# Layer-0 scores by query strips: 32 queries of four heads to a product, in place of 128 queries of one head

## The chip, the cores and the metric

The kernel runs on one core of a Trainium2 chip. A core has a matrix engine (TensorE, PE in the profile; its weight loads stand apart as PEld), a vector engine (VectorE, DVE), a scalar engine (ScalarE, ACT), a general engine (GpSimd, POOL) and a queue engine (SyncE, SP) that issues most transfers here. Engines work through their own instruction queues in order and wait for each other by semaphores. TensorE reads its operands from SBUF and writes to PSUM banks; of a matmul's two operands one is loaded first (the stationary one, `lhsT`), the other (the moving one, `rhs`) streams past it. The metric is the time of one execution on the device, in microseconds.

## What is computed

Two transformer layers over 1024 tokens of 512 features, each with an attention part and a feed-forward part, with layer norms, shifts, scales and gates around them. Only the first layer's attention bears on the change. It has 32 query heads and 8 key/value heads of 128 features, four query heads to one key/value head:

```python
q = _dequant_matmul(hidden_states, qw_q, scales_q).reshape(b, s, NH, HD).transpose(0, 2, 1, 3)
k = _dequant_matmul(hidden_states, qw_k, scales_k).reshape(b, s, NKV, HD).transpose(0, 2, 1, 3)
v = _dequant_matmul(hidden_states, qw_v, scales_v).reshape(b, s, NKV, HD).transpose(0, 2, 1, 3)
q = _apply_rope(q, cos, sin)
k = _apply_rope(k, cos, sin)
k = jnp.repeat(k, rep, axis=1)
v = jnp.repeat(v, rep, axis=1)
scores = jnp.einsum('bhqd,bhkd->bhqk', q, k) / math.sqrt(HD)
causal = jnp.tril(jnp.ones((s, s), dtype=bool))
scores = jnp.where(causal[None, None], scores, jnp.finfo(scores.dtype).min)
attn = jax.nn.softmax(scores.astype(jnp.float32), axis=-1).astype(q.dtype)
ctx = jnp.einsum('bhqk,bhkd->bhqd', attn, v)
ctx = ctx.transpose(0, 2, 1, 3).reshape(b, s, NH * HD)
return _dequant_matmul(ctx, qw_o, scales_o)
```

All of it is in float32; the weights come as small integers with scales and are made into floats on the core. The mask is causal: query i sees keys 0 to i.

## The kernel before

Layer 0's attention is a loop over 8 groups `g` (one key/value head and its four query heads) and, in each, over the 8 query blocks `qi` of 128 queries, in the order 7, 0, 6, 1, 5, 2, 4, 3 (in the last group 3, 7, 2, 6, 1, 5, 0, 4). One pair (g, qi) is a step; there are 64. A step works on the keys up to the block's end, n = qi + 1 blocks of 128, so it has 128(qi + 1) key columns.

A step first calls `head_probs(u, r)` for the four heads r (L314 to L336). For a head, TensorE multiplies the 128 queries of the block with all key columns, in pieces of up to 512 (L320), into a PSUM tile `sc` of two banks, of which there are three. VectorE adds the causal mask `cmask` to the last 128 columns (L325), and takes the negated maximum of each row (L327). ScalarE takes the exponential with the row's sum (L330), VectorE the reciprocal (L335), and ScalarE scales by it (L336). The probabilities stand in one wide tile `pr` for all four heads. `transpose_probs` (L338) then transposes it in squares of 32 x 32, a quarter at a time (L342), and 16 transfers on SP's queue (L344) put the pieces together in `pT`, keys on partitions. `pr` and `pT` have one buffer each for the large blocks (qi from 4 on) and one for the small.

Two steps later `context` (L349) multiplies `pT` with the values, 128 keys at a time, for the four heads at once (L353), ScalarE copies the result to `ctxT` (L359), and `project_o` multiplies it with the output weights (L364), VectorE applies the gate (L369) and GpSimd adds to the tokens (L370). In the program these stand after heads 1 and 3 of the step in hand (`drain`).

`side_work(g, i)` prepares the next group during step i: weights are loaded and made into floats by VectorE (`dequant`, L218), and `project_k`, `project_v`, `project_q` multiply them with the layer-normed tokens `hT`. `project_rope` (L229) does a head in two halves of 512 tokens: four matmuls (L234), three VectorE products with cosine and sine (L240, L242, L243), and a GpSimd addition (L244) that writes the half of the rotated head. Step 3 projects heads 0 and 1 of the next group, step 5 head 2, step 7 head 3. Each head has its own tile `qT` of 128 x 1024, eight of them in rotation:

```python
qp = st.enter_context(tc.tile_pool(name="a0q", bufs=8))
...
qT[h] = qp.tile([P, S], F32, tag="qT", name="qT")
project_rope(qT[h], wf.pop(("q", h)))
```

The lines give each engine's work in program order; when the program is built, instructions of different engines and, within an engine, of neighbouring parts are interleaved, so that for instance a context matmul can stand ahead of scores that stand above it in the source. What follows from that on the chip is fixed: each engine runs its list in order. A float32 matmul appears in the profile as two records, with two weight loads.

Of the kernel before, what the change touches and what calls it, by code (L numbers as in the profile page):

```python
# [9 lines left out]
F32 = mybir.dt.float32  # L10
# [3 lines left out]
ALU = mybir.AluOpType  # L14
AX = mybir.AxisListType
PSUM = bass.MemoryType.PSUM

P = 128
S = 1024
# [4 lines left out]
NEG = -1e30  # L24
# [3 lines left out]
REP = NH // NKV  # L28
# [14 lines left out]
def block_kernel(ctx: ExitStack, tc: tile.TileContext, a: dict, out: bass.AP):  # L43
    nc = tc.nc

    const = ctx.enter_context(tc.tile_pool(name="const", bufs=1))
# [18 lines left out]
    def psum_mm():  # L65

        return psA[0].tile([P, 512], F32, tag="mm", name="mm")
# [23 lines left out]
    make_identity(nc, ident)  # L91
    cmask = const.tile([P, P], F32, tag="cmask", name="cmask")
    make_causal_mask(nc, cmask, mask_val=NEG)
    eps_t = const.tile([P, 1], F32, tag="eps", name="eps_t")
    nc.vector.memset(eps_t, EPS)

# [93 lines left out]
    with ExitStack() as st:  # L190
# [7 lines left out]
            hT = layernorm_mod(hp, mod[0, 0], mod[0, 1])  # L198
        wp = st.enter_context(tc.tile_pool(name="a0w", bufs=3))
        kvp = st.enter_context(tc.tile_pool(name="a0kv", bufs=2))  # L200
        qp = st.enter_context(tc.tile_pool(name="a0q", bufs=8))
        rp = st.enter_context(tc.tile_pool(name="a0r", bufs=2))
        pp = st.enter_context(tc.tile_pool(name="a0p", bufs=1))
        tmp_open(st, "a0", bufs=2)
# [4 lines left out]
        B = 32  # L209
        NB = P // B  # L210
# [18 lines left out]
        def project_rope(dst, wf):  # L229

            for half in range(2):
                ps = psum_mm()
                for c in range(NC):
                    nc.tensor.matmul(  # L234
                        ps, lhsT=wf[:, c, :], rhs=hT[half][:, c, :],
                        start=(c == 0), stop=(c == NC - 1),
                    )
                sl = bass.ts(half, 512)
                t1 = rp.tile([P, 512], F32, tag="t1", name="t1")
                nc.vector.tensor_mul(t1, ps, cosT[:, sl])  # L240
                t2 = rp.tile([P, 512], F32, tag="t2", name="t2")
                nc.vector.tensor_mul(t2[0:64, :], ps[64:128, :], sinT[64:128, sl])  # L242
                nc.vector.tensor_mul(t2[64:128, :], ps[0:64, :], sinT[0:64, sl])  # L243
                nc.gpsimd.tensor_tensor(dst[:, sl], t1, t2, ALU.add)  # L244

        kT, vv, qT, wo, wf = {}, {}, {}, {}, {}
# [6 lines left out]
        def project_k(g):  # L253
            kT[g] = kvp.tile([P, S], F32, tag="kT", name="kT")
            project_rope(kT[g], wf.pop(("k", g)))
# [23 lines left out]
            vv[g], vv[g + 1] = v[:, :, :HD], v[:, :, HD:]  # L279

        def project_q(h):
            qT[h] = qp.tile([P, S], F32, tag="qT", name="qT")
            project_rope(qT[h], wf.pop(("q", h)))

        def load_o_weight(g):
            w = wp.tile([P, REP, D], F32, tag="wo", name="wo", bufs=2)
# [9 lines left out]
        class Step:  # L296


            def __init__(self, g, qi):
                self.g, self.qi, self.n = g, qi, qi + 1  # L300
                size = "big" if qi >= NT // 2 else "small"
                cap = NT if qi >= NT // 2 else NT // 2
                shape = [P, NB * REP * cap * B]
                used = NB * REP * self.n * B
                pr = pp.tile(shape, F32, tag=f"pr{size}", name="pr")
                pT = pp.tile(shape, F32, tag=f"pT{size}", name="pT")


                self.pr, self.pT = (
                    t[:, :used].rearrange("p (b r k i) -> p b r k i", b=NB, r=REP, i=B)  # L310
                    for t in (pr, pT)
                )

        def head_probs(u, r):  # L314

            nk = u.n * P
            ps = sp.tile([P, S], F32, tag="sc", name="sc")
            for n0 in range(0, nk, 512):
                w = min(512, nk - n0)
                nc.tensor.matmul(  # L320
                    ps[:, n0 : n0 + w], lhsT=qT[u.g * REP + r][:, bass.ts(u.qi, P)],
                    rhs=kT[u.g][:, n0 : n0 + w], start=True, stop=True,
                )
            dg = ps[:, u.qi * P : nk]
            nc.vector.tensor_tensor(dg, dg, cmask, ALU.add)  # L325
            nb = small.tile([P, 1], F32, tag="nb", name="nb")
            nc.vector.tensor_reduce(nb, ps[:, :nk], AX.X, ALU.max, negate=True)  # L327
            rs = small.tile([P, 1], F32, tag="rs", name="rs")
            pr = u.pr[:, :, r, :, :]
            nc.scalar.activation(  # L330
                pr.rearrange("p b k i -> p k b i"),
                ps[:, :nk].rearrange("p (k b i) -> p k b i", b=NB, i=B),
                AF.Exp, bias=nb, accum_out=rs,
            )
            nc.vector.reciprocal(rs, rs)  # L335
            nc.scalar.activation(pr, pr, AF.Copy, scale=rs)  # L336

        def transpose_probs(u):  # L338

            for b in range(NB):  # L340
                t = u.pr[:, b, :, :, :].rearrange("p r k i -> p (r k i)")
                nc.vector.transpose(t, t)  # L342
                for q in range(NB):
                    nc.sync.dma_start(  # L344
                        u.pT[b * B : (b + 1) * B, q, :, :, :].rearrange("p r k i -> p (r k i)"),
                        t[q * B : (q + 1) * B, :],
                    )

        def context(u):  # L349

            ps = psum_mm()
            for kj in range(u.n):
                nc.tensor.matmul(  # L353
                    ps, lhsT=vv[u.g][:, kj, :],
                    rhs=u.pT[:, :, :, kj, :].rearrange("p a r i -> p r a i"),
                    start=(kj == 0), stop=(kj == u.n - 1),
                )
            u.ctxT = rp.tile([P, REP, P], F32, tag="ctxT", name="ctxT")
            nc.scalar.copy(u.ctxT.rearrange("p r q -> p (r q)"), ps)  # L359
# [12 lines left out]
        def side_work(g, i):  # L372

            if g + 1 == NKV:
                if i in (1, 3):
                    mod_chunk(1, 3 + i // 2)
                elif i == 5:
                    mod_chunk(1, 5)
                return
            h0 = (g + 1) * REP  # L380
            if i == 0:
                load_k(g + 1)
            elif i == 1:
                project_k(g + 1)
                load_q(h0)
            elif i == 2:
                if (g + 1) % 2 == 0:
                    project_v(g + 1)
                load_q(h0 + 1)
            elif i == 3:  # L390
                project_q(h0)
                project_q(h0 + 1)
                load_q(h0 + 2)
            elif i == 4:
                load_q(h0 + 3)
                if g == 3:
                    mod_prepare(1)
                for l, j in ([(0, 3 + g)] if g < 3 else [(1, g - 4)] if g > 3 else []):
                    mod_chunk(l, j)
            elif i == 5:  # L400
                project_q(h0 + 2)
            elif i == 6:
                load_o_weight(g + 1)
            else:
                project_q(h0 + 3)
# [16 lines left out]
        def drain(u, part):  # L422
            if u is not None:
                (context if part == 0 else project_o)(u)

        for g in range(NKV):
            last = g == NKV - 1
            order = (3, 7, 2, 6, 1, 5, 0, 4) if last else (7, 0, 6, 1, 5, 2, 4, 3)
            for i, qi in enumerate(order):
                u = Step(g, qi)  # L430
                old = behind.pop(0) if len(behind) == 2 else None
                for r in range(REP):
                    head_probs(u, r)
                    if r % 2:
                        drain(old, r // 2)
                transpose_probs(u)
                behind.append(u)
                side_work(g, i)
        for u in behind:
            context(u)  # L440
            project_o(u)
# [5 lines left out]
    st = ctx.enter_context(ExitStack())  # L447
# [7 lines left out]
    def bank():  # L455
        return sp.tile([P, 512], F32, tag="sc", name="sc")
# [53 lines left out]
    with ExitStack() as f0:  # L510
# [55 lines left out]
        for j in range(NF):  # L566
            for b in range(2):
                pgu = []
                for m in range(2):
                    ps = bank()  # L570
                    for c in range(NC):
                        nc.tensor.matmul(  # L572
                            ps, lhsT=gu[:, j, m, c, :], rhs=hTc[b][:, c, :],
                            start=(c == 0), stop=(c == NC - 1),
# [70 lines left out]
    B = 32  # L645
# [506 lines left out]
```

## Time and profile before

| | us |
|---|---|
| median of three runs | 1970.83 |
| the three runs | 1971.68, 1970.83, 1964.02 |
| the profiled execution | 1969.94 |
| its span, first to last instruction | 1968.2 |

| engine | busy, us | share of the span |
|---|---|---|
| TensorE, matmul | 1848.3 | 94% |
| TensorE, weight loads | 871.5 | 44% |
| VectorE | 1178.6 | 60% |
| ScalarE | 667.5 | 34% |
| GpSimd | 225.5 | 11% |

The mean granted clock of TensorE is 0.967 of full speed. Layer 0's attention ends near 1150 us; after it come layer 0's feed-forward part and layer 1.

How to read the rows shown below: a row of instructions gives the line, the engine, the operation, output<-input by the program's names (`sc` scores, `nb` negated maximum, `mm` a PSUM tile of the projections), shapes and count, then busy time and the mean duration of one in ns, then the idle time of the engine before these instructions and what ended it. A row of the timeline gives start and length in us, and in brackets the idle time before it. Busy time of TensorE has the latency of each record in it, so that records that follow each other closely overlap: how far they stand apart is read from starts.

### The profile page before, as it was taken

How to read it: one execution, taken by the hardware profiler on the slowest of the kernel's cores; microseconds unless marked ns; L12 is line 12 of the kernel's file. 1: busy time of each engine (PE TensorE's matmuls, PEld its weight loads, DVE VectorE, ACT ScalarE, POOL GpSimd, SP SyncE). 2: the span in 40 equal slices, each digit the busy share in tenths (PEclk: the TensorE clock that was granted, in tenths of full speed). 3: DMA queues.
4: the chain of work that ended last, by engine and by line, in shares of the span. 5: the costliest groups of instructions: out<-in, count | busy, mean ns of one | idle time of the engine just before them, and what ended most of it. 6: DMA issues, size and time to landing. Idle time of an engine off the chain costs nothing.

```text
span 1968.2 us, 21006 instructions
## 1 busy us (share of the span) xinstructions
PE 1848.3 (94%) x6550; PEld 871.5 (44%) x6550; DVE 1178.6 (60%) x2638; ACT 667.5 (34%) x1392; POOL 225.5 (11%) x192
## 2 busy tenths in 40 slices
PE   4989999999999999999998879999988999999987
PEld 3434454444544444544443434444554444333434
DVE  5766756677566777566776542323456667677432
ACT  1134424434334344244335410000113323354520
POOL 0211111111111111111210110002000000000010
PEclk9989999999999999999999989999999889999999
DMA  5344435345533444353444360001001000000001
GB/s 198 107 111 137 120 99 137 90 128 148 128 89 83 114 141 115 106 136 93 126 127 96 86 239 0 0 0 48 0 2 63 10 8 7 4 7 8 4 11 38
DMA packets 93424, 155.77 MB, mean 79 GB/s; under 512 B 25056, under 2 KB 37984, under 8 KB 93312
## 3 DMA queue, kind: packets, MB, share of 16 engines
q1 hardware_dynamic: 92432, 151.53, 28.6%
q0 software_dynamic: 880, 2.88, 0.4%
q8 instruction: 53, 0.87, 0.2%
q14 instruction: 59, 0.48, 0.1%
HBM read 74.38 MB, written 2.36 MB: 39 GB/s over the span
## 4 chain that ended last, share of the span: by engine, by line
PE 74%; DVE 14%; DMA 3%; ACT 3%; issue 2%; SPq 1%; POOL 1%; DVEq 0%; POOLq 0%; ACTq 0%
PE mm L234 12%; PE mm L364 10%; PE mm L353 9%; PE sc L320 8%; PE sc L572 8%; PE sc L756 5%; PE sc L805 4%; PE sc L591 4%; PE ctx L829 3%; DVE q L767 2%; PE sc L666 2%; DVE nb L327 2%; PE mm L274 2%; PE sc L974 1%; DMA os<-in_s_o_dram 1%
## 5 line engine op out<-in xcount | busy, mean ns | idle before, releaser
L330 ACT ACTIVATE pr<-sc,nb 128x1024 f32<-128x1024 f32 (+7 forms) x256 | 188.2, 737 | 416.7 <-DVE nb L327 243.4
L234 PE MATMUL mm<-hT,wf 128*128 128x512 f32 x640 | 284.1, 595 | 8.3 <-ACT wf L251 6.4
L353 PE MATMUL mm<-pT,v 128*128 128x512 f32 x576 | 267.3, 610 | 21.0 <-DMA pT<-pr 21.0
L320 PE MATMUL sc<-kT,qT 128*128 128x512 f32 (+3 forms) x768 | 275.6, 490 | 7.4 <-ACT pr L330 7.4
L364 PE MATMUL mm<-wo,ctxT 128*128 128x512 f32 x512 | 237.7, 603 | 11.4 <-ACT ctxT L359 11.2
L320 PEld LDWEIGHTS sc<-kT,qT 128*128 128x128 f32 x768 | 139.5, 191 | 159.1 <-issue 126.1
L336 ACT ACTIVATE pr<-pr,rs 128x1024 f32<-128x1024 f32 (+7 forms) x256 | 188.3, 771 | 50.0 <-DVE rs L335 49.7
L234 PEld LDWEIGHTS mm<-hT,wf 128*128 128x128 f32 x640 | 121.6, 191 | 159.6 <-issue 144.6
L327 DVE TENSOR_REDUCE nb<-sc 128x1 f32<-128x1024 f32 (+7 forms) x256 | 187.7, 751 | 3.5
L342 DVE STREAM_TRANSPOSE pr<-pr 128x1024 f32<-128x1024 f32 (+7 forms) x256 | 177.7, 747 | 19.8 <-ACT pr L336 19.2
L818 ACT ACTIVATE pspace<-sc 128x512 f32<-128x512 f32 (+3 forms) x303 | 127.0, 505 | 168.3 <-PE sc L812 120.3
L353 PEld LDWEIGHTS mm<-pT,v 128*128 128x128 f32 x576 | 111.3, 196 | 148.9 <-issue 144.0
L756 PE MATMUL sc<-kv,q 32*128 32x512 f32 (+3 forms) x768 | 157.5, 550 | 11.0 <-DVE mx L767 9.5
L767 DVE CUSTOM_DVE_ANT_0 q<-sc,cwide 128x512 f32<-128x512 f32 (+3 forms) x256 | 125.5, 490 | 67.4 <-PE sc L756 42.6
L370 POOL TENSOR_TENSOR x<-x,ot 128x512 f32<-128x512 f32 x64 | 83.2, 1299 | 669.2 <-DVE ot L369 576.6
L572 PE MATMUL sc<-hT,gu 128*128 128x512 f32 x352 | 153.1, 594 | 0.0
L364 PEld LDWEIGHTS mm<-wo,ctxT 128*128 128x128 f32 x512 | 94.6, 191 | 128.1 <-issue 92.3
L805 PE MATMUL sc<-q,kv 32*128 32x512 f32 (+3 forms) x768 | 111.5, 583 | 4.2 <-DVE mx L772 2.0
L244 POOL TENSOR_TENSOR qT<-t,t 128x512 f32<-128x512 f32 x64 | 87.6, 1368 | 182.5 <-DVE t L243 182.5
L335 DVE RECIPROCAL rs<-rs 128x1 f32<-128x1 f32 x256 | 37.7, 157 | 114.0 <-ACT pr L330 113.2
L572 PEld LDWEIGHTS sc<-hT,gu 128*128 128x128 f32 x352 | 66.2, 190 | 85.2 <-issue 79.6
L772 DVE TENSOR_REDUCE mx<-sc 128x1 f32<-128x512 f32 x128 | 79.2, 681 | 37.1 <-PE sc L756 37.1
(166 smaller groups left out, 1755.3 us busy)
## 6 DMA issues: line engine op xcount, KB each, us to landing
pT<-pr SPq DMA_DIRECT2D x128, 128.0 KB, 2.3
pT<-pr SPq DMA_DIRECT2D x128, 112.0 KB, 2.2
wm<-in_wmodT_dram SPq DMA_DIRECT2D x48, 256.0 KB, 2.8
pT<-pr SPq DMA_DIRECT2D x128, 96.0 KB, 2.1
pT<-pr SPq DMA_DIRECT2D x128, 80.0 KB, 2.1
wi<-in_qw_q_dram SPq DMA_DIRECT2D x32, 256.0 KB, 4.1
ws<-in_s_q_dram SPq DMA_DIRECT2D x32, 256.0 KB, 3.8
oi<-in_qw_o_dram SPq DMA_DIRECT2D x32, 256.0 KB, 3.5
```

Source lines behind the costliest of these rows:

```text
L234: nc.tensor.matmul(ps, lhsT=wf[:, c, :], rhs=hT[half][:, c, :], start=(c == 0), stop=(c == NC - 1),)
L320: nc.tensor.matmul(ps[:, n0 : n0 + w], lhsT=qT[u.g * REP + r][:, bass.ts(u.qi, P)], rhs=kT[u.g][:, n0 : n0 + w], start=True, stop=True,)
L327: nc.vector.tensor_reduce(nb, ps[:, :nk], AX.X, ALU.max, negate=True)
L330: nc.scalar.activation(pr.rearrange("p b k i -> p k b i"), ps[:, :nk].rearrange("p (k b i) -> p k b i", b=NB, i=B), AF.Exp, bias=nb, accum ...
L336: nc.scalar.activation(pr, pr, AF.Copy, scale=rs)
L342: nc.vector.transpose(t, t)
L353: nc.tensor.matmul(ps, lhsT=vv[u.g][:, kj, :], rhs=u.pT[:, :, :, kj, :].rearrange("p a r i -> p r a i"), start=(kj == 0), stop=(kj == u.n ...
L364: nc.tensor.matmul(ps, lhsT=u.ctxT[:, r, :], rhs=wo[u.g][:, r, :], start=(r == 0), stop=(r == REP - 1),)
L572: nc.tensor.matmul(ps, lhsT=gu[:, j, m, c, :], rhs=hTc[b][:, c, :], start=(c == 0), stop=(c == NC - 1),)
L756: nc.tensor.matmul(banks[r][:, at : at + w], lhsT=u.q[kp, bass.ts(i, P)], rhs=kT1[kp, u.g, n0 : n0 + w], start=True, stop=True,)
L767: nc.vector.tensor_tensor_reduce(sm[:, :w], ps, cwide[:, 512 - w :], 1.0, -3e38, ALU.add, ALU.max, accum_out=u.mx[:, i, r, 0:1],)
L805: nc.tensor.matmul(banks[r][:, :w], lhsT=kT1[kp, u.g, bass.ts(kb, P)], rhs=u.q[kp, q0:QW], start=True, stop=not diag,)
```

## The change

The scores of a step are made by query strips in place of heads. One product now has, as its 128 rows, 32 queries of each of the group's four heads; a step has four strips `s`. A strip's products end with the keys of its own queries, at column 128qi + 32(s + 1), where before each head's went to the end of the block.

- `qT` is one tile per group, 128 x 32 x 4 x 32 (features; strips of 32 queries over all 1024; heads; queries), with two in rotation. The tile is as large as four of the old ones. GpSimd's addition (now L252) writes a head into it in runs of 32.
- `probs(u, s)` takes the place of `head_probs(u, r)`: the matmuls (L332) end at `d0 + B`; VectorE sets the rest of the block's columns to -1e30 (L336, three strips of four), adds a 128 x 32 mask `cmask4` to the strip's own 32 columns (L338) and takes the maximum over the columns up to there (L340). Exponential (L343), reciprocal (L348) and scaling (L349) work on the block's full width, as before.
- `cmask4` is made once at the start, by four small VectorE copies out of `cmask`.
- `pr` and `pT` hold the same numbers in another order. `transpose_probs` issues the same number of transposes (L355) and transfers of the same size; context matmuls (L366) read `pT` in runs of 128.
- The calls stand in the same places: strips 1 and 3 are followed by `drain`, where heads 1 and 3 were.

The core of the diff:

```diff
+    cmask4 = const.tile([P, 32], F32, tag="cmask4", name="cmask4")
+    for r in range(REP):
+        rows = slice(32 * r, 32 * r + 32)
+        nc.vector.tensor_copy(cmask4[rows, :], cmask[rows, rows])
...
-        qp = st.enter_context(tc.tile_pool(name="a0q", bufs=8))
+        qp = st.enter_context(tc.tile_pool(name="a0q", bufs=2))
...
+                if len(dst.shape) == 3:
+                    t1, t2 = (t.rearrange("p (b i) -> p b i", i=B) for t in (t1, t2))
+                    sl = bass.ts(half, 512 // B)
                 nc.gpsimd.tensor_tensor(dst[:, sl], t1, t2, ALU.add)
...
-            qT[h] = qp.tile([P, S], F32, tag="qT", name="qT")
-            project_rope(qT[h], wf.pop(("q", h)))
+            g, r = divmod(h, REP)
+            if r == 0:
+                qT[g] = qp.tile([P, S // B, REP, B], F32, tag="qT", name="qT")
+            project_rope(qT[g][:, :, r, :], wf.pop(("q", h)))
...
-        def head_probs(u, r):
+        def probs(u, s):
             nk = u.n * P
+            d0 = u.qi * P + B * s
             ps = sp.tile([P, S], F32, tag="sc", name="sc")
-            for n0 in range(0, nk, 512):
-                w = min(512, nk - n0)
+            q = qT[u.g][:, NB * u.qi + s, :, :].rearrange("p r i -> p (r i)")
+            for n0 in range(0, d0 + B, 512):
+                w = min(512, d0 + B - n0)
                 nc.tensor.matmul(
-                    ps[:, n0 : n0 + w], lhsT=qT[u.g * REP + r][:, bass.ts(u.qi, P)],
-                    rhs=kT[u.g][:, n0 : n0 + w], start=True, stop=True,
+                    ps[:, n0 : n0 + w], lhsT=q, rhs=kT[u.g][:, n0 : n0 + w], start=True, stop=True
                 )
-            dg = ps[:, u.qi * P : nk]
-            nc.vector.tensor_tensor(dg, dg, cmask, ALU.add)
+            if s + 1 < NB:
+                nc.vector.memset(ps[:, d0 + B : nk], NEG)
+            dg = ps[:, d0 : d0 + B]
+            nc.vector.tensor_tensor(dg, dg, cmask4, ALU.add)
             nb = small.tile([P, 1], F32, tag="nb", name="nb")
-            nc.vector.tensor_reduce(nb, ps[:, :nk], AX.X, ALU.max, negate=True)
+            nc.vector.tensor_reduce(nb, ps[:, : d0 + B], AX.X, ALU.max, negate=True)
             rs = small.tile([P, 1], F32, tag="rs", name="rs")
-            pr = u.pr[:, :, r, :, :]
+            pr = u.pr[:, :, :, s, :]
             nc.scalar.activation(
-                pr.rearrange("p b k i -> p k b i"),
-                ps[:, :nk].rearrange("p (k b i) -> p k b i", b=NB, i=B),
+                pr.rearrange("p j k i -> p k j i"),
+                ps[:, :nk].rearrange("p (k j i) -> p k j i", j=NB, i=B),
                 AF.Exp, bias=nb, accum_out=rs,
             )
...
-                    rhs=u.pT[:, :, :, kj, :].rearrange("p a r i -> p r a i"),
+                    rhs=u.pT[:, :, kj, :, :],
...
-                for r in range(REP):
-                    head_probs(u, r)
-                    if r % 2:
-                        drain(old, r // 2)
+                for s in range(NB):
+                    probs(u, s)
+                    if s % 2:
+                        drain(old, s // 2)
```

## The prediction

> **What bounds the kernel now.** I read the table of engines by stage first, since the change touches only layer 0's attention loop, which runs from 87 to about 1150 us. Its columns are the stretch, its length, busy time and instructions of TensorE (PE), its weight loads, VectorE (DVE), ScalarE (ACT) and GpSimd (POOL), the granted clock, and the DMAs:
>
> ```profile
> 87.00:150.00 63.00, 56.23 (x134) 25.47 (x133) 44.92 (x93) 26.50 (x52) 10.40 (x8) 0.92 0.40 98
> 150.00:1016.00 866.00, 851.62 (x2213) 409.93 (x2212) 596.90 (x1217) 347.30 (x697) 151.49 (x116) 1.00 0.45 118
> 1016.00:1150.00 134.00, 112.01 (x265) 50.45 (x264) 72.21 (x166) 55.76 (x108) 14.42 (x11) 0.94 0.38 93
> ```
>
> In the 866 us in the middle TensorE idles for 14.4 us and VectorE for 269: there each microsecond of TensorE is one of the kernel, and VectorE work is hidden. At the start (6.8 us of idle) and in the last group (22.0 us) the chain matmul, mask, maximum, exponential, transpose, DMA sets the pace. Then the places where a group's first scores follow its last q projection, in the chain of waits (start, length, what) and in the timeline of the same place:
>
> ```profile
> 346.45 6.87 PE mm L234 x16
> 353.32 3.43 PE sc L320 x8
> 356.75 4.29 PE mm L353 x10
> ...
> 353.43 0.69 DVE L240 TENSOR_TENSOR t<-mm,cosT 128x512 f32<-128x512 f32 x1 [0.84 <-PE mm L234]
> 354.13 0.69 DVE L242 TENSOR_TENSOR t<-mm,sinT 64x512 f32<-64x512 f32 x1
> 354.84 0.68 DVE L243 TENSOR_TENSOR t<-mm,sinT 64x512 f32<-64x512 f32 x1
> 355.60 1.27 POOL L244 TENSOR_TENSOR qT<-t,t 128x512 f32<-128x512 f32 x1 [1.68 <-DVE t L243]
> ```
>
> Call T = 353.32 us the end of the projection of the next group's fourth head. TensorE goes straight on with heads 0 and 1, while head 3's second half is still being rotated; its qT is whole at 356.87, T+3.55. The six places of this kind between 150 and 900 us show the same offsets to 0.02 us. Last, the rows that give prices:
>
> ```profile
> L320 PE MATMUL sc<-kT,qT 128*128 128x512 f32 x384 | 188.5, 597 | 4.0 <-ACT pr L330 4.0
> L325 DVE TENSOR_TENSOR sc<-sc,cmask 128x128 f32<-128x128 f32 x256 | 68.8, 288 | 54.3 <-PE sc L320 53.4
> L327 DVE TENSOR_REDUCE nb<-sc 128x1 f32<-128x1024 f32 x32 | 39.1, 1222 | 0.8
> L327 DVE TENSOR_REDUCE nb<-sc 128x1 f32<-128x896 f32 x32 | 34.2, 1087 | 0.5
> L749 DVE MEMSET mx<- 128x32 f32 x8 | 0.6, 85 | 0.0
> ```
>
> **What TensorE saves.** One matmul is two records, and eight 512-column records take 3.43 us, so 0.429 us a record, 0.86 a matmul, 1.68 ns a column (the 597 ns are a record's latency, not its spacing). A step's four heads took 4 x 128(qi+1) columns; its four query strips take 32, 64, 96 and 128 columns behind 4 x 128qi: 192 fewer, 0.322 us. In six of the eight query blocks the narrowed pieces keep 160 columns or more, and I count that in full: 7 groups x 6 x 0.322 = 13.5 us. In blocks 0 and 4 the pieces have 32 to 96 columns. The narrowest records of this loop have 128 (four in 0.44 us, 0.11 each), so nothing shows that narrower ones come faster: 0 at one end, 8 x 2 x 0.322 = 5.2 us at the other; a loss is excluded, as the operands only shrink. I take 0, since each piece still loads 128 weight columns. The last group's 1.9 us lie beside a chain that paces it; 0 to 1.9, I take 0.6.
>
> The Trainium skill speaks against this change here: "TensorE: Matmul & The Clock Gate", section "LDWEIGHTS (loading the stationary operand)", gives the load as the number of weight columns over 1.2 in ns, 107 ns for 128. By that rule the 5.2 us are nothing; by the columns alone they are had.
>
> **What the change adds on TensorE: a wait.** The stationary operand now holds four heads, so a group's first scores need head 3's rotation, which before only its fourth product needed. In the changed program's order the first scores after the last q projection wait for GpSimd's write of head 3's second half, at groups 1 to 6, and TensorE has one context matmul (0.86 us) to do first. It then stands from T+0.86 to T+3.6: 2.74 us, six times, 16.4 us. Behind the waiting matmul on TensorE's queue stand the second strip's scores, four more context matmuls and the out projection; nothing of them is pulled ahead. Is it absorbed? From 353.32 to 367.75 scores, context and out projection follow without a gap, so there is no idle to take it. VectorE's chain comes later by less (first strip done at T+3.6+1.56, maximum begun near T+5.7 against T+4.0 before), so it doesn't add.
>
> At group 0 the same wait meets the paced start. qT is whole there at 91.24 us (GpSimd 89.48 + 1.76); 928 columns take 1.56, memset and mask 0.45, so the maximum begins at about 93.3 where it began at 90.36: 3.0 us, between 0 (taken out of the 2.63 and 3.90 us that TensorE idles at 108 and 115 us) and 4.5 (scores at half clock); I take 3.0, because those idles hang on this very chain. At the last group only the first half is needed (query block 3), ready 0.8 us after the projection: 0 to 0.8, I take 0.5.
>
> **What the idle does to the clock.** 2.10 us of idle ending at 601.28 were followed by this (same columns as above; 0.51 is the granted clock):
>
> ```profile
> 602.60:606.10 3.50, 3.50 (x6) 1.34 (x5) 0.84 (x1) 0.48 (x1) 0.00 (x0) 0.51 0.19 43
> ```
>
> The idles of 2.63 and 3.90 us at 108 and 115 us were followed by half clock too; those of 1.6 us and less between 300 and 900 us were not. A half-clock stretch here is 3.4 us and so costs 1.7 us of TensorE. The stretches fall on a raster of 3.4 us, and an idle of 2.74 that a border splits badly escapes: I take two in three, 6 x 2/3 x 1.7 = 6.7 us; ends 0 and 10.2.
>
> The same page of the skill ("Why this matters for your kernels") asks for idle gaps over about 3 us before the clock drops. By that rule the six waits cost no clock and the sum is 6.7 us lower. The trace's 2.10 us decide against it.
>
> **VectorE, GpSimd, the rest.** The mask shrinks from 128 to 32 columns: at (1222-1087)/128 = 1.05 ns a column 0.10 us less, four times a step; the maxima lose 192 columns, 0.20 us. Three memsets of 96, 64 and 32 columns in PSUM come in, each waiting for its strip's matmul: between 0.085 (the 128x32 memset) and 0.288 (the mask on 128 columns). I take the mask's row less its columns, as it works on the same bank: 0.25, 0.22, 0.19. A step: +0.66 - 0.40 - 0.20 = +0.06 us; 64 steps, 4 us, hidden behind TensorE in the middle. In the last group, without that cover, 0.5 us; at the upper price 8 x 0.27 = 2.2, at the lower a gain of 2.8. GpSimd writes qT in 16 runs of 32 instead of one of 512: 1.27 us as now, at most its slowest 1.77, which would lengthen the six waits by 3.0 us in all; I take 0. The exponential wrote runs of 32 already; the scaling now does too, and at 128x1024 the two rows stand at 1115 and 1140 ns: nothing, under ScalarE's 60% idle. Transposes, their 16 DMAs a step and SP's queue keep count and size. The four copies for the small mask run on VectorE before its inputs have landed: nothing; unhidden, below 0.5 us.
>
> **Sum.** -13.5 - 0.6 + 16.4 + 3.0 + 0.5 + 6.7 + 0.5 = +13.0 us. The profiled execution took 1969.94 us (span 1968.2), 0.9 below the median 1970.83. 1969.94 + 13.0 = 1983 us.
>
> **Rivals.** (a) The wait counts, the clock stays: +6.3, 1976 us. For it: no idle of exactly this length is in the trace. Against: 2.10 us sufficed once. (b) Slower still: GpSimd's runs cost 0.5 us each and the memsets their upper price, on top of the forecast (+3.0 + 1.7, and half clock at every wait, +3.5): 1991 us. For: both prices are unseen. Against: both nearest rows are cheap. (c) Not slower: the exponential's chain, not TensorE, paces the steps behind each boundary, so that a boundary costs only the chain's 1.7 us, the narrow pieces save in full and the clock holds: -13.5 - 5.2 - 1.9 + 10.2 + 3.0 = -7.4, 1962.5 us. It decides once a boundary costs under 13.5 / 6 = 2.25 us. Against it: the gapless 14 us behind T and 1.7% idle. (d) That scores aren't trimmed is out: the built program has widths 416, 448, 480, 512.
>
> **Chances.** Forecast 0.57, (a) 0.20, (b) 0.15, (c) 0.08. With bounds, 1968 to 1994 us holds eight in ten; the forecast's own range is 1977 to 1989. A measurement tells no change from about 0.5%, 9.9 us, so under 1961 is faster and over 1980.7 slower. Part of the forecast (0.05) and most of (a) and (c) fall between: faster 0.06, same 0.29, slower 0.65.
>
> **What would show it.** Six waits of about 2.7 us of the scores' matmul for GpSimd's qT; half clock behind most of them; score matmuls some 14 us less between 150 and 1016 us; records of 32 to 96 columns no closer than 0.11 us; memsets of 0.19 to 0.25 us. Waits under 2 us, or other work moved into them, make the forecast wrong to the fast side; waits for the maximum in mid-loop, to the slow side.

## The result, and the profile after

| | before | after |
|---|---|---|
| median, us (six runs each on one chip) | 1971.01 | 1993.49 |
| lowest to highest | 1964.02 to 1973.22 | 1990.24 to 2000.76 |
| profiled execution, us | 1969.94 | 1991.92 |
| its span, us | 1968.2 | 1990.1 |
| ratio of times | | 1.0129, interval 1.0111 to 1.0148 |

The change made the kernel slower by 22.5 us between the medians, or 1.3% by the ratio of times. The forecast was 13 us, 1983. The direction held; the size did not.

The same table of engines by stage as before, now of the changed kernel (stretch, length, busy time and instructions of TensorE, its loads, VectorE, ScalarE and GpSimd, granted clock, DMAs):

```profile
87.00:150.00 63.00, 50.48 (x121) 23.06 (x120) 39.26 (x99) 26.41 (x52) 8.17 (x7) 0.92 0.41 99
150.00:1016.00 866.00, 832.09 (x2175) 401.86 (x2174) 582.81 (x1335) 335.96 (x675) 153.58 (x116) 0.99 0.43 114
1016.00:1150.00 134.00, 120.50 (x295) 54.91 (x294) 80.79 (x221) 64.22 (x127) 14.41 (x11) 0.96 0.42 106
```

In the middle stretch TensorE now idles 33.9 us where it idled 14.4. (The last group starts later than before, so the third row holds other work than it did.)

What TensorE waited for, from the list of waits (engine, line, what it waited for: us in total, times, longest), first before, then after:

```profile
PE mm L353 <- DMA pT<-pr: 21.0, 5, 7.5
PE mm L364 <- ACT ctxT L359: 11.2, 17, 2.1
PE sc L320 <- ACT pr L330: 7.4, 7, 2.6
```

```profile
PE sc L332 <- POOL qT L252: 21.2, 8, 3.2
PE mm L377 <- ACT ctxT L372: 16.8, 26, 2.0
PE mm L366 <- DMA pT<-pr: 16.5, 5, 7.4
PE sc L332 <- ACT pr L343: 12.6, 11, 4.5
```

One wait is new, the scores' for GpSimd's qT. Two have grown by over 5 us each: that of the out projection for the context's copy, and that of the scores for the exponential, which frees their PSUM tile. The new wait stands in the timeline of the boundary that the prediction took as its example (start, length, what, idle before):

```profile
361.81 1.26 POOL L252 TENSOR_TENSOR qT<-t,t 128x512 f32<-128x512 f32 x1 [3.56 <-DVE t L248]
362.80 1.02 PE L366 MATMUL mm<-pT,v 128*128 128x512 f32 x2
...
364.48 0.68 DVE L248 TENSOR_TENSOR t<-mm,sinT 64x512 f32<-64x512 f32 x1
365.19 0.69 DVE L223 SCALAR_TENSOR_TENSOR wf<-wi,ws 128x512 f32<-128x512 int32 x1
365.24 1.76 POOL L252 TENSOR_TENSOR qT<-t,t 128x512 f32<-128x512 f32 x1 [2.17 <-DVE t L248]
367.06 3.43 PE L332 MATMUL sc<-kT,qT 128*128 128x512 f32 x8 [3.24 <-POOL qT L252]
```

T is 362.80 here. One context matmul follows, as forecast; then TensorE stands until GpSimd has written the second half of the fourth head. By the starts the scores come at T+4.26 and not at T+3.6: the addition took 1.76 us, where the first half of the same head, written in the same runs of 32, took 1.26.

To see where the 22 us are, I took the attention loop of each trace apart, from the first score matmul to the first matmul behind the last out projection. Records that follow closely stand 0.838 ns a column apart (0.429 us for 512); that is counted as work, the rest of each spacing as idle, and inside stretches of half clock up to the work's own length again as clock.

| us | before | after |
|---|---|---|
| start, to the first score | 87.5 | 93.1 |
| loop | 1066.0 | 1082.3 |
| of it work (scores) | 995.4 (247.1) | 973.1 (226.5) |
| clock | 13.2 | 16.5 |
| idle | 57.4 | 92.7 |
| of it context to scores | 0.6 | 22.0 |
| scores to out projection | 12.9 | 21.4 |
| scores to scores | 5.9 | 16.9 |
| scores to context | 13.8 | 10.5 |
| all after the loop | 814.7 | 814.8 |

The span grew by 21.9: 5.6 at the start, 16.3 in the loop. The scores' work fell by 20.6 us (all work by 22.3, as four records of a projection moved ahead of the first score), half clock cost 3.3 more, and idle rose by 35.3. The six boundaries make 20.2 of that, in 20.4 us of gaps (five of 3.40 us and one of 3.13, behind which half clock blurs the reading, taken as 3.4). Leave the boundaries and the two short ones at the first and last group out, and some 14 us of new idle remain, two thirds of the saved columns. Of these 14, 3.3 are the narrow pieces, whose records of 32 to 96 columns come slower than 0.838 ns a column. Some 6 stand between scores in the first and last group, where scores wait for the exponential, and 8.5 between scores and out projections; elsewhere, ahead of the contexts above all, idle fell by some 4.

How saved columns turn into a wait is seen at one out projection in the third group, in a step of 768 key columns, in both timelines. Before:

```profile
428.83 1.45 PE L320 MATMUL sc<-kT,qT 128*128 128x512 f32 x4
429.07 0.94 ACT L336 ACTIVATE pr<-pr,rs 128x768 f32<-128x768 f32 x1 [0.23 <-DVE rs L335]
429.92 0.57 ACT L359 COPY ctxT<-mm 128x512 f32<-128x512 f32 x1
...
430.54 3.70 PE L364 MATMUL mm<-wo,ctxT 128*128 128x512 f32 x8 [0.25 <-ACT ctxT L359]
```

After:

```profile
441.63 1.45 PE L332 MATMUL sc<-kT,qT 128*128 128x512 f32 x4
442.19 0.93 ACT L349 ACTIVATE pr<-pr,rs 128x768 f32<-128x768 f32 x1 [0.23 <-DVE rs L348]
443.03 0.57 ACT L372 COPY ctxT<-mm 128x512 f32<-128x512 f32 x1
...
443.65 3.70 PE L377 MATMUL mm<-wo,ctxT 128*128 128x512 f32 x8 [0.56 <-ACT ctxT L372]
```

The copy of the context stands on ScalarE behind the third exponential and its scaling, and these behind the masks and maxima on VectorE, which start when VectorE has finished the rotation ahead of them (its last product ends at 422.17 before and 435.29 after). From there to the start of the copy it is 7.75 us before and 7.74 after: the chain is as long as it was. The last scores, ahead of it on TensorE, are done sooner: they start 6.66 us behind the rotation before and 6.34 after, less by the 0.32 that a step saves. From their start to the end of the copy it is 1.66 us before and 1.97 after, so TensorE waits 0.56 us in place of 0.25.

But not all 8.5 us are of this kind. At the out projection of query block 3, in groups 0 to 5, the program as built has another order. Before, six score records stand between the context and the out projection; after, two. The place in the second group, before, then after:

```profile
368.19 3.60 PE L353 MATMUL mm<-pT,v 128*128 128x512 f32 x8
371.63 1.47 PE L320 MATMUL sc<-kT,qT 128*128 128x128 f32 x6
372.93 1.45 PE L364 MATMUL mm<-wo,ctxT 128*128 128x512 f32 x3
```

```profile
380.97 3.65 PE L366 MATMUL mm<-pT,v 128*128 128x512 f32 x8
384.46 0.36 PE L332 MATMUL sc<-kT,qT 128*128 128x96 f32 x2
385.30 2.84 PE L377 MATMUL mm<-wo,ctxT 128*128 128x512 f32 x6 [0.48 <-ACT ctxT L372]
```

By the starts TensorE idles 0.68 us there in place of nothing, six times, 4.1 us in all. With the columns put back (`e3`, below) the order at this place is that of the changed kernel and the idle is still 0.62 us. So about half of the growth at the out projections came from the order that the change brought with it, and not from columns saved.

### The profile page after: what moved, and what is told of

The parts are those of the page before. It is cut to its first block, busy times and chain, and to the rows that moved or that the text cites. A ratio compares the mean times of both kernels' runs of the same rounds, so it can differ in the third digit from the quotient of the medians.

```text
span 1990.1 us, 21179 instructions
## 1 busy us (share of the span) xinstructions
PE 1843.4 (93%) x6550; PEld 869.8 (44%) x6550; DVE 1175.8 (59%) x2834; ACT 666.8 (34%) x1392; POOL 227.0 (11%) x192
## 4 chain that ended last, share of the span: by engine, by line
PE 69%; DVE 16%; ACT 5%; DMA 4%; issue 3%; POOL 2%; SPq 2%; DVEq 0%; POOLq 0%; ACTq 0%
PE mm L377 10%; PE mm L239 8%; PE mm L366 8%; PE sc L585 8%; PE sc L332 8%; PE sc L769 5%; PE sc L818 4%; PE sc L604 4%; PE ctx L842 4%; PE sc L679 2%; PE mm L282 2%; DVE q L780 2%; DVE nb L340 2%; ACT pr L349 2%; SPq L357 2%
## 5 line engine op out<-in xcount | busy, mean ns | idle before, releaser
L343 ACT ACTIVATE pr<-sc,nb 128x1024 f32<-128x1024 f32 (+7 forms) x256 | 187.7, 736 | 442.0 <-DVE nb L340 318.9
L332 PE MATMUL sc<-kT,qT 128*128 128x512 f32 (+15 forms) x768 | 268.2, 479 | 33.9 <-POOL qT L252 21.2
L366 PE MATMUL mm<-pT,v 128*128 128x512 f32 x576 | 265.9, 605 | 16.5 <-DMA pT<-pr 16.5
L332 PEld LDWEIGHTS sc<-kT,qT 128*128 128x128 f32 x768 | 141.2, 194 | 189.8 <-issue 125.3
L349 ACT ACTIVATE pr<-pr,rs 128x1024 f32<-128x1024 f32 (+7 forms) x256 | 188.8, 769 | 42.2 <-DVE rs L348 41.2
L355 DVE STREAM_TRANSPOSE pr<-pr 128x1024 f32<-128x1024 f32 (+7 forms) x256 | 177.0, 746 | 18.8 <-ACT pr L349 16.9
L340 DVE TENSOR_REDUCE nb<-sc 128x1 f32<-128x384 f32 (+31 forms) x256 | 176.1, 702 | 3.9
L366 PEld LDWEIGHTS mm<-pT,v 128*128 128x128 f32 x576 | 110.0, 194 | 139.6 <-issue 136.2
L769 PE MATMUL sc<-kv,q 32*128 32x512 f32 (+3 forms) x768 | 157.4, 550 | 11.2 <-DVE mx L780 9.7
L377 PEld LDWEIGHTS mm<-wo,ctxT 128*128 128x128 f32 x512 | 93.1, 191 | 132.3 <-issue 92.7
L252 POOL TENSOR_TENSOR qT<-t,t 128x512 f32<-128x512 f32 x64 | 90.0, 1406 | 189.5 <-DVE t L248 189.5
L348 DVE RECIPROCAL rs<-rs 128x1 f32<-128x1 f32 x256 | 39.0, 158 | 108.4 <-ACT pr L343 105.6
```

Source lines behind the costliest of these rows:

```text
L332: nc.tensor.matmul(ps[:, n0 : n0 + w], lhsT=q, rhs=kT[u.g][:, n0 : n0 + w], start=True, stop=True)
L340: nc.vector.tensor_reduce(nb, ps[:, : d0 + B], AX.X, ALU.max, negate=True)
L343: nc.scalar.activation(pr.rearrange("p j k i -> p k j i"), ps[:, :nk].rearrange("p (k j i) -> p k j i", j=NB, i=B), AF.Exp, bias=nb, accum ...
L366: nc.tensor.matmul(ps, lhsT=vv[u.g][:, kj, :], rhs=u.pT[:, :, kj, :, :], start=(kj == 0), stop=(kj == u.n - 1),)
L377: nc.tensor.matmul(ps, lhsT=u.ctxT[:, r, :], rhs=wo[u.g][:, r, :], start=(r == 0), stop=(r == REP - 1),)
L769: nc.tensor.matmul(banks[r][:, at : at + w], lhsT=u.q[kp, bass.ts(i, P)], rhs=kT1[kp, u.g, n0 : n0 + w], start=True, stop=True,)
```

## The experiments

Three sets were run, each on one chip beside the kernel before; comparisons between sets go by the ratio to it. The two kernels that were measured in two sets (`e1` and `h1`, `e7` and `h7`) came out 4 and 6 us apart, so a difference between sets is uncertain by about as much. In the expectations, W is the theory that the boundary waits are most of the loss, and "given back" (C) that the saved columns were turned into other waits.

### The wait taken away: the fourth head projected a step earlier

`e1_q3_early` is the changed kernel with head 3 of the next group projected at step 6, ahead of the load of the output weights, and not at step 7:

```diff
             elif i == 6:
+                project_q(h0 + 3)
                 load_o_weight(g + 1)
-            else:
-                project_q(h0 + 3)
```

> The changed kernel with the projection of the next group's fourth head one step earlier (step 6 in place of 7), so that its rotation is long done when the next group's first scores want it. Theory W (the loss is the wait at the group boundaries, six times 3.4 us, with its half clock): the waits for qT go at groups 1 to 6, 20 to 24 us less than the changed kernel's 1993.5, about 1971 us, level with the kernel before. Rival N (the strips' longer VectorE chain, memset, mask, maximum, paces the loop, and TensorE would stand at another place if not here): no more than 5 us less, above 1988 us.

Measured: 1960.84 us, ratio 0.9968 (0.9953 to 0.9983). A second measurement in the third set, `h1_q3_early_again`, gave 1966.95, 0.9989 (0.9976 to 1.0003), above the 0.995 to 0.998 that was expected of it:

> The strips with the fourth head projected a step earlier, trimmed columns, unaltered: 0.995 to 0.998 by every theory. With the next it says how much of 20.6 us of columns counts without the boundary waits: 8 to 12 us by the loop's length in the profiles (10.1), 12 to 20 us by the first ratios (0.0081).

The changed kernel itself, measured again (`e9_after_again`):

> The changed kernel unaltered, beside the three others of this set, so that they are compared on one chip. Every theory expects the ratio of the first measurement, 1.0111 to 1.0148, and 6 waits of about 3.2 us of the score matmul for GpSimd's qT.

It came to 1989.73 us, 1.0122 (1.0109 to 1.0135). So the move takes off 30 us by its first measurement and 26 by its second, each give or take 4, where theory W gave 20 to 24. In the loops of the two profiles of either kernel, 1082.3 and 1083.6 against 1059.4 and 1065.8, it is 20.4 us on average; the first score came 1.6 us earlier, within the scatter of the start (below). The timeline of a boundary now:

```profile
352.58 3.70 PE L377 MATMUL mm<-wo,ctxT 128*128 128x512 f32 x8
...
356.12 2.47 PE L332 MATMUL sc<-kT,qT 128*128 128x416 f32 x6
...
358.43 4.45 PE L366 MATMUL mm<-pT,v 128*128 128x512 f32 x10
```

Out projection, scores and context stand close on each other, and the list of waits holds qT once, with 1.0 us, at the very start. The boundary waits are shown to be the largest part of the loss; by the times the move brought rather more than their 20.4 us, and what the rest is stays open.

The control, the kernel before with the same move (`e2_before_q3_early`):

> The same move of the projection in the kernel before, as a control. Theory W: the kernel before has no such wait, so nothing is gained, 1967 to 1975 us. If moving the projection is worth something by itself (it shortens the last step of each group), this shows it: under 1963 us.

1966.0 us, 0.9994 (0.9978 to 1.0009): nothing. The move repairs something that only the changed kernel has.

### The columns put back

`e3_full_width` is the changed kernel with all score matmuls as wide as before; masks, maxima and layout stay as changed:

```diff
-            for n0 in range(0, d0 + B, 512):
-                w = min(512, d0 + B - n0)
+            for n0 in range(0, nk, 512):
+                w = min(512, nk - n0)
```

> The changed kernel with its score matmuls on all the block's keys again (the memset then overwrites what is masked), all else kept: it undoes the columns saved and nothing else. If saved columns count in full: 8 groups of 2.58 us less what the narrow pieces didn't give, 18 us more than the changed kernel, 2011 us. Theory C (a good part of the columns is given back as wait for the context's copy, because fewer columns stand between a step's context and its out projection): 6 to 10 us more, 2000 to 2004 us.

1998.27 us, 1.0151 (1.0134 to 1.0169). Against the changed kernel's 1.0122 that is 5.7 us, give or take 4.3, at the low end of theory C's 6 to 10; the loop is 1090.4 against 1082.3 and 1083.6, 7.5 us more, though 20.6 us of work were put back. So of the columns saved about a third came out as time in this arrangement, by the interval of the times anything up to a half. 12 us of idle went away as the work returned (92.8 to 80.6), and of it 4.8 between scores and out projection, 5.1 between scores and scores (about half of it the narrow pieces' slower records) and 2.9 at the boundaries.

One reservation: the edit does not only put columns back. When the program is built, the order of TensorE's list changes with it, at 44 of the loop's 2604 places. At three of the six boundaries two context products, not one, now stand ahead of the waiting scores, and the gap is 2.54 us in place of 3.40. These 2.6 us are order and not columns. At the out projections the order is the same in both, and there 5.0 us of idle went: at query block 6, for instance, 0.73 us became 0.07, four times.

Without the boundary waits the same edit, `f1_q3_early_full_width`:

> The changed kernel with the fourth head projected a step earlier (so without the six boundary waits), and all score matmuls at full width again: 20.6 us of TensorE's columns come back. Theory 'given back' (the columns saved were mostly followed by a longer wait of the out projection for the copy of the context, whose chain through the exponential did not get shorter): only 4 to 9 us more than the same arrangement with trimmed columns, whose ratio was 0.9968, so 0.999 to 1.001, with the idle between scores and out projection falling from 18.0 us to some 12 to 14. Theory 'in full' (only the boundary waits spoilt the forecast, the columns count as they were costed): 14 to 20 us more, 1.004 to 1.007, and that idle as it was.

1974.9 us, 1.0049 (1.0036 to 1.0062), 15.9 us over the first measurement of its partner, give or take 3.9, which is what 'in full' gave; but the loops of the two profiles were only 10.1 us apart, and the idle between scores and out projection fell from 18.0 to 15.4, neither as it was nor to 12 to 14. Since times and profiles disagreed, the pair was run again side by side, `h2_q3_early_full_width_again` beside `h1` above:

> The same with full-width score matmuls: 1.001 to 1.003 if the loop's length in the two profiles is right (10 us over the kernel above), 1.004 to 1.006 if the first ratios are (16 us).

1974.54 us, 1.0036 (1.0022 to 1.0049): 9.3 us over its partner, give or take 3.8 (7.6 between the medians), by its ratio between the two expectations. The loops were 1069.9 and 1065.8. The trimmed kernel's own loop differed by 6.4 us between its two profiles (4.0 of it clock), so one profile can't size this. Taken together the columns are worth 9 to 16 us here by the times and 4 to 10 by the loops, out of the 17 that remain of 20.6 once the narrow pieces' loss (below) is taken off. That this is more than beside the boundary waits (5.7 and 7.5) is what the times suggest and the loops don't. The lists of waits of `h1`, then of `h2`:

```profile
PE mm L377 <- ACT ctxT L372: 19.3, 29, 2.0
PE mm L366 <- DMA pT<-pr: 17.0, 6, 7.4
PE sc L332 <- ACT pr L343: 13.6, 11, 4.5
```

```profile
PE mm L366 <- DMA pT<-pr: 19.7, 6, 7.5
...
PE mm L377 <- ACT ctxT L372: 13.1, 23, 2.0
PE sc L332 <- ACT pr L343: 11.7, 8, 3.4
```

The trimmed kernel waits 6.2 us longer for the context's copy and 1.9 for the exponential. Here too the order differs (64 places), but at the out projections little of the difference hangs on it: by the starts 0.7 us of 8.0 stand where the order is another.

### The out projection made later

If the out projection's wait takes the columns, then a step's context should be projected later, when its copy has long been made. `e7_q3_early_late_o` is `e1` with this in the loop:

```diff
-                    if s % 2:
-                        drain(old, s // 2)
+                    if s == 1:
+                        if ready:
+                            project_o(ready.pop())
+                        if old is not None:
+                            context(old)
+                            ready.append(old)
```

> The first of these kernels with the out projection of a step issued one step later, beside the next step's context, so that the copy of the context is long done. Theory C: the waits of the out projection for that copy, 2.7 us a group, go: 12 to 20 us less than the first of these kernels, about 1955 us. Rival: ScalarE's chain paces the steps, and the wait comes back at the scores: within 4 us of it.

1956.71 us, 0.9936 (0.9911 to 0.9960): 6.3 us less than `e1`, give or take 5.6, between the two expectations. And again in the third set:

> The partner of the kernel above with trimmed columns, unaltered from before: ratio 0.991 to 0.996 by every theory.

1950.01 us, 0.9907 (0.9890 to 0.9925), the best seen, and 16.1 us less than `h1`, give or take 4.3, as theory C had it. Both profiles have the same loop, 1049.5 and 1049.7 us. The waits of the second:

```profile
PE mm L366 <- DMA pT<-pr: 27.0, 8, 11.9
...
PE sc L332 <- ACT pr L343: 8.6, 5, 4.5
```

The out projection's wait for the context's copy is down to 0.7 us. Idle between scores and out projection fell from 18.0 to 4.9 us in the first pair; the contexts' wait for the transposed probabilities rose from 17 to 26 us, so part moved there. The control, `e7b_before_q3_early_late_o`, is the kernel before with both moves:

> The kernel before with both moves of the best arrangement so far (fourth head projected a step earlier, out projection a step later), as a control. If the moves bring as much to either layout, the ratio is that of the strips with them against the strips with the first move alone, about 0.995 (10 us of loop). If the out projection's wait came from the shorter strips (1.03 us a group before, 2.7 after), the kernel before gains less, at most the 4 to 6 us of that idle: 0.997 to 1.000, and the strips stay ahead by 4 us or more.

1960.87 us, 0.9978 (0.9968 to 0.9987). Its loop, 1061.7 us, is 5.3 shorter than with the first move alone; the strips' loop shrank by 9.9 and 16.1. The strips with both moves are ahead of this control by 8 us (give or take 5) or 14 us (4). By the times the later out projection is worth 3.1 us to the kernel before (give or take 3.6) and 6.3 or 16.1 to the strips; the first isn't apart from the 3.1, the second is, and the loops agree with it. So it is probably worth more to the strips, as theory C has it, and the strips are the better layout once the order suits them.

Then the columns put back in this arrangement too:

> The strips with the fourth head projected a step earlier and the out projection a step later, with all score matmuls at full width: 20.6 us of columns come back where the out projection no longer waits for the copy of the context. Theory 'given back at the out projection': here the columns count nearly in full, 13 to 18 us more than the same kernel with trimmed columns, and more than the pair without the late out projection shows in this set. Rival, that another wait takes them (the transposed probabilities' transfers, the exponential that frees the score tile): 5 to 10 us, no more than that pair.

1962.03 us, 0.9970 (0.9956 to 0.9983): 12.4 us over its partner `h7`, give or take 4.4; the loop is 1063.6, 13.9 over. That misses the expectation by a little, and against 9.3 in the pair with the early out projection it is the right way round but not apart from it. The loops say 14 against 4 to 10. That the columns count for more where the out projection doesn't wait is thus likely and not proved by the times.

### The start

`g1_best_prologue` is `e7` with the four mask copies behind the layer norm and `project_v(0)` behind the first queries:

```diff
-        project_v(0)
         for r in range(REP):
...
+        project_v(0)
```

> The strips with the fourth head projected a step earlier and the out projection a step later (0.9936 before), and two moves at the start: the four small mask copies after the layer norm, and the first values projected behind the first queries. If the 5 us that the start lost hang on the copies (0.65 us) and on the first scores' wait for the fourth head, the values' matmuls fill that wait: the first scores' wait for qT (1.00 us) goes, the first maximum begins 2 to 4 us earlier than 95.4, ratio 0.991 to 0.993. If the start is paced by the weights' landing and rotation on VectorE instead, nothing changes beyond the 0.65 us: 0.993 to 0.995.

1953.35 us, 0.9944 (0.9928 to 0.9960): no gain over `e7` in the times. Its first maximum begins at 94.02 us, but that says little: in the ten profiles of strips with the unaltered start it begins anywhere from 93.2 to 95.4. The first scores no longer wait for qT, because they now stand behind the values' matmuls.

## Why the prediction was wrong in size

By its own steps, against spans (forecast +13.0, measured +21.9):

| term | forecast | measured | from |
|---|---|---|---|
| columns, all groups | -14.1 | -7.5 | loops of after and `e3` |
| boundary waits | +16.4 | +20.4 | gaps in the trace |
| start | +3.0 | +5.6 | first score |
| half clock | +6.7 | +3.3 | loop's clock, after less before |
| last group, VectorE | +1.0 | not read apart | |
| sum | +13.0 | +21.8 | |

The measured terms come from different comparisons, so that they close within 0.1 us is partly luck: by the ratios the columns are worth 5.7 us, give or take 4.3, `e3` has another order at three boundaries, and part of the start's 5.6 is scatter between executions.

**The failed step is "I count that in full".** The prediction argued that from 353.32 to 367.75 us scores, context and out projection followed without a gap, "so there is no idle to take it". That looked at one stretch of 14 us. Elsewhere TensorE already stood at the out projection for the context's copy, 17 times and 11.2 us in all; the prediction says nothing of this wait. It is the end of a chain over VectorE and ScalarE whose length, where it was followed, the change left alone (7.75 and 7.74 us), so columns saved ahead of it lengthen the wait. Idle between scores and out projection rose from 12.9 to 21.4 us; 4.1 of this is the other order at query block 3, which the prediction didn't price either. The first group's 1.9 us of columns were counted in full too, beside a chain that the prediction itself said sets the pace there; scores waiting for scores and for the exponential grew there and in the last group. `e3` shows the sum: 20.6 us of columns put back cost 5.7 to 7.5, where the forecast counted 14.1. How the shortfall divides between chain and order is known in part only. The second term that was mis-sized is the boundary waits, below: 4.0 us.

**The narrow pieces** were taken as saving nothing, with 5.2 us as the other end. The starts of their records say less than half: two records of 32 columns take 28 + 111 ns, of 64 56 + 111, of 96 83 + 111, of 128 109 + 111. The second record of a pair, behind which the operand changes, is followed no sooner than 0.11 us, and where a pair of 64 follows a pair of 32 (seven of the eight steps of block 0) its first record takes 138. That 138 + 111 is more than a pair of 128 columns took, so the prediction's "a loss is excluded" doesn't hold for each piece. In all it is 0.16 of 0.322 us in nine steps and 0.08 in seven, about 2 us of 5.2. The Trainium skill, "TensorE: Matmul & The Clock Gate", section "LDWEIGHTS (loading the stationary operand)", gives 107 ns for loading 128 columns. The 111 ns are near it for one record of two; that every record is held to it, as the prediction read it, those of 28 to 83 ns contradict.

**The boundary waits** were right in number, place, cause and what stands ahead of them; their price was 3.40 us, not 2.74. GpSimd's addition of the second half took 1.76 us at each, the upper price that the prediction named and put into rival (b) alone, and it began 0.16 us later (T+2.44 against T+2.28). Runs of 32 are not the reason: the first half, in the same runs, took 1.26. What differs is which engine was first. In the kernel before, the addition at 355.60 that the prediction took as its row had the same dequantization beside it:

```profile
355.75 1.66 DVE L218 SCALAR_TENSOR_TENSOR wf<-wi,ws 128x512 f32<-128x512 int32 x1
```

It began 0.15 us behind the addition, the addition took 1.27 us, and the dequantization 1.66 in place of the 0.69 that it takes alone. After the change it stands on VectorE right behind the rotation, no longer behind the first mask, and begins first (365.19, against 365.24): it takes 0.69 and the addition 1.76. In the two traces 55 additions have a dequantization beside them. In the 31 where the dequantization began first the addition took 1.58 to 1.78 us; in the 24 where the addition began first it took 1.26 to 1.27, and the dequantization 1.10 to 1.70. There is no exception, but no run moved the dequantization to test it.

**Half clock** followed 3 of the 6 waits, against two in three forecast. Windows right behind two of them (columns as above):

```profile
221.50:224.90 3.40, 3.40 (x5) 1.59 (x6) 0.22 (x2) 0.00 (x0) 0.00 (x0) 0.55 0.42 101
367.10:370.50 3.40, 3.40 (x9) 1.75 (x10) 1.45 (x3) 0.00 (x0) 0.00 (x0) 1.00 0.49 116
```

In the second profile of the changed kernel it was 5 of 6. The mechanism and the odds held; one stretch that the kernel before had, at 602.7 us, was gone, so that the net is half the term. The Trainium skill's page that the prediction weighed ("TensorE: Matmul & The Clock Gate", "Why this matters for your kernels") asks for idle over about 3 us: with the gaps of 3.4 us that came, this would be half clock behind each, and the traces show it behind three and five of six.

**VectorE** got 14 us cheaper in mask, maximum and memset where 4 us more was forecast, and in the middle stretch it had 283 us of idle to hide it in. The rows (line, operation, count, busy us, mean ns):

```profile
L336 DVE MEMSET sc<- 128x96 f32 (+2 forms) x192 | 20.0, 112 | 55.5 <-PE sc L332 53.8
```

```profile
L340 DVE TENSOR_REDUCE nb<-sc 128x1 f32<-128x384 f32 (+31 forms) x256 | 176.1, 702 | 3.9
L338 DVE TENSOR_TENSOR sc<-sc,cmask 128x32 f32<-128x32 f32 x256 | 46.1, 194 | 33.0 <-PE sc L332 29.9
```

The memsets cost 0.14, 0.11 and 0.09 us for 96, 64 and 32 columns, not the 0.25 to 0.19 of the mask's row; the masks fell by 22.7 us and the maxima by 11.6.

**The start** lost 5.0 us to the first maximum in these two profiles, not 3.0. But from the gate's transposes, which stand just ahead of the first scores, to the first maximum it is 3.33 us in all three profiles of the layout by heads, and 6.59 in all six of trimmed strips with this start: 3.26 us for the wait, close to the forecast. The other 1.8 us lie ahead of that. The prediction put the mask copies before their inputs had landed; the timeline shows them in the layer norm's way:

```profile
9.90 0.71 DVE L98 COPY cmask<-cmask 32x32 f32<-32x32 f32 x4
10.65 0.18 DVE L163 RECIPROCAL rstd<-rstd 128x4 f32<-128x4 f32 x1
...
93.06 4.29 PE L332 MATMUL sc<-kT,qT 128*128 128x512 f32 x10 [1.00 <-POOL qT L252]
...
95.39 1.12 DVE L340 TENSOR_REDUCE nb<-sc 128x1 f32<-128x928 f32 x1
```

The first normed tile begins 0.63 us later here. The rest is within the scatter: the gate's transposes begin between 86.6 and 88.8 us in the ten profiles of strips with this start, and between 87.0 and 88.5 in the three by heads.

Of the rivals, (a) fell with the half clock that came, and (c) with the waits' full price; its idea, that a chain and not TensorE takes columns, was right in part, though at the out projections and not behind the boundaries. (b) had the waits' price right for a reason that was not the one, and its memsets wrong.

## What to carry to other kernels

A bound engine that is 98% busy still ends some of its waits on chains that don't shrink with its work: before counting saved work in full, follow what each small, repeated wait hangs on, since the saving goes there first. Putting several producers into one operand makes the consumer wait for the last of them, so move the last producer earlier in the same change; here that one move took 26 to 30 us off, and with the out projection a step later the layout that had lost 1.3% gained 0.6 to 0.9% (0.4 to 0.7% against the kernel before with the same two moves). A probe that puts back one part of the change (here full-width products) tells what that part is worth better than its share of busy time, but only as far as the program as built keeps its order: compare the lists of instructions before reading the difference.

## What the runs showed of the hardware that was not expected

- A float32 matmul's two records are not spaced alike when they are narrow: with 32 columns the first takes 28 ns and the second 111, and the first of 64 columns behind them 138.
- Half clock is no sharp function of the idle: of six gaps of about 3.4 us three were followed by it in one execution, five in another, while the kernel before met it once behind 2.10 us.
- A GpSimd addition of 128x512 and a VectorE dequantization beside it did not share the delay: whichever began first took its usual time (1.26 and 0.69 us) and the other was longer (up to 1.78 and 1.70), in 55 cases of 55.
- A VectorE memset in PSUM cost 0.09 to 0.14 us for 32 to 96 columns, under half of an addition there on 128 columns (0.288).
